# A graph layer's one-hot matrices: a third of the weight products on GpSimd, compare numbers in PSUM, three buffers

## The chip, the core and the metric

The kernel runs on one core of a Trainium2 chip. The metric is the device time of one execution in microseconds. The kernel before takes 516.95 us, the median of three runs (513.53 to 521.79).

## The reference, cut to what matters

There are 2048 nodes with 256 features and 67584 edges sorted by `dst`. The first layer sums weighted, normalised node rows over the edges; the second is a mixture of eight experts with two experts a token. The change touches only the first.

```python
edge_index = jnp.stack([src, dst])
# first layer: row = src, col = dst
gathered = edge_weight[:, None] * layernorm(x)[dst]
x = x + segment_sum(gathered, src, 2048) + node_vec1
# second layer: x + sum over the 2 best of 8 experts of weight * (gelu(LN(xt) @ W1) @ W2)
x = x + ffn(layernorm(x))
```

## The kernel before, in words

The kernel turns the edge sum into matrix products. It builds the weighted adjacency matrix, 2048 by 2048 in fp32, in slices of 64 `dst` nodes, and multiplies it with the normalised rows.

**Finding the edges.** The nodes are taken in 1024 pairs, 128 pairs to a round `q`, eight rounds. For each pair a GpSimd gather (L219, three of them: `win_s`, `win_d`, `win_w`) fetches the window of 128 edges that starts at the first edge of the pair; another gather (L200, `run`) and a ScalarE count (L209) find that start. VectorE makes two keys out of an edge (L252 to L255): its `src` modulo 128, and a number from 0 to 31 out of the `src` block and which of the two nodes it points at. TensorE transposes keys and weights (L263, L264), so that an edge of the window lies on each partition; ScalarE writes them out twice side by side as bf16 (`k2`, `w2`, L266 and L269). The fp32 weight is split into three bf16 parts, by subtractions on VectorE (L280) and casts on ScalarE (L281); `w2` holds the three parts.

**One-hots and the product.** A step `n`, of 32, takes 32 pairs, four steps to a round. `make_hots(n)` works on VectorE: L290 compares the first key with 0 to 127 and gives `hl` (128 partitions by 32 pairs by 128), L293 compares the second key with 0 to 31 and gives `eq` (32 by 32), and L297 multiplies `eq` with the three parts of the weight and gives `hr` (32 by 3 by 32). The numbers that are compared with are `iota_b`, bf16 in SBUF. `make_cols(n)` multiplies `hr` with `hl` on TensorE (L317, 96 products of 32 by 128, three adding up in PSUM), ScalarE copies the result out (L320), a DMA writes it to DRAM (L321), and every second step a DMA reads 128 `dst` nodes back as `ac` (L324). `dense` (L331) multiplies four such `ac` with the normalised rows, 16 fp32 matmuls for two blocks of output rows, and VectorE adds the result to `acc` (L336).

**Order.** All five engines run a list written out by hand (`manual_schedule`), each in its order. Step `n` of the loop issues `make_hots(n + 1)` first, then work for later rounds (L280 where `n % 4` is 0 or 1, L214 and L215 and the gathers where it is 1, L252 to L255 where it is 3), then the additions (L336) of the `dense` of the step before, then `make_cols(n)` and from `n = 9` on one `dense`, two at the end of a group of eight. `hl`, `eq` and `hr` have two buffers each, the product `pa` has three PSUM banks. GpSimd's queue holds only gathers in this stage. After the loop follow the last `dense` products, the routing of the tokens and the experts (L886 to L956), which the change leaves alone.

Of the kernel before, what the change touches and what calls it, by code (L numbers as in the profile page):

```python
# [9 lines left out]
F32 = mybir.dt.float32  # L10
BF16 = mybir.dt.bfloat16
# [3 lines left out]
OP = mybir.AluOpType  # L15
AX = mybir.AxisListType
PSUM = bass.MemoryType.PSUM
DRAM = bass.MemoryType.DRAM

P = 128  # L20
# [4 lines left out]
def kernel(  # L25
# [30 lines left out]
    nc = tc.nc  # L56
# [10 lines left out]
    RK = NB * GC  # L67
    GB = P // GC
    GH = GB // 2
# [19 lines left out]
    gnn = ctx.enter_context(ExitStack())  # L89
# [63 lines left out]
    iota_b = consts.tile([P, P], BF16, name="iota_b")  # L153
# [16 lines left out]

    cols_1 = gnn.enter_context(tc.tile_pool(name="cols_1", bufs=CB))
    ps_s = gnn.enter_context(tc.tile_pool(name="ps_s", bufs=2, space=PSUM))
    edges = gnn.enter_context(ExitStack())
    cols_0 = edges.enter_context(tc.tile_pool(name="cols_0", bufs=CB))
    pool = lambda name, bufs, **k: edges.enter_context(tc.tile_pool(name=name, bufs=bufs, **k))
# [51 lines left out]
    def block_stats(bn, mv, t, blocks):  # L227
        for b in blocks:
# [3 lines left out]

    prep = pool("prep", 2)
    keys = pool("keys", 3)
    hotl = pool("hotl", 2)
    hotr = pool("hotr", 2)
    rowsp = pool("rowsp", 3)
    ps_k = pool("ps_k", 1, space=PSUM)
    ps_a = pool("ps_a", 3, space=PSUM)
    two = lambda t, g, n: t[:, g * GH:(g + 1) * GH, None, :].to_broadcast([P, GH, n // 2, 2])  # L240
    pair = lambda n: iota_b[:, None, :n].rearrange("p o (n t) -> p o n t", t=2) \
                                        .to_broadcast([P, GH, n // 2, 2])
    parts = {}

# [39 lines left out]
    def make_hots(n):  # L284


        k2, w2, _ = parts[n // 4]
        g = n % 4
        hl = hotl.tile([P, GH, P], BF16, name="hl")
        nc.vector.tensor_tensor(hl.rearrange("p g (n t) -> p g n t", t=2),  # L290
                                two(k2[:, 0], g, P), pair(P), OP.is_equal)
        eq = hotr.tile([P, GH, RK], BF16, name="eq")
        nc.vector.tensor_tensor(eq.rearrange("p g (n t) -> p g n t", t=2),  # L293
                                two(k2[:, 1], g, RK), pair(RK), OP.is_equal)
        hr = hotr.tile([P, GH, 3, RK], BF16, name="hr")
        w = w2[:, g * GH:(g + 1) * GH].rearrange("p g i t -> p (g i) t")
        nc.vector.tensor_tensor(  # L297
            hr.rearrange("p g i (n t) -> p (g i) n t", t=2),
            eq[:, :, None, :].to_broadcast([P, GH, 3, RK]),
            w[:, :, None, :].to_broadcast([P, GH * 3, RK // 2, 2]), OP.mult)  # L300
        return hl, hr

    def make_cols(n, hl, hr):
# [37 lines left out]
    with tc.manual_schedule(engines=ALL):  # L341
# [24 lines left out]
        next_part(0, 2)  # L366
        turn_keys(1, f1)
        hots = {0: make_hots(0)}
        late = []
        NH = 2 * NB  # L370
        for n in range(NH):
            q = n // 4
            if n + 1 < NH:
                hots[n + 1] = make_hots(n + 1)
# [17 lines left out]
            g, k = divmod(n - 2 * CB - 1, 2 * CB)  # L392
# [14 lines left out]
            if n == 1:  # L407
# [4 lines left out]
                o = 0  # L412
# [10 lines left out]
                o = 0  # L423
# [68 lines left out]
    with tc.If(n_used < E):  # L492
# [11 lines left out]
        with tc.tile_pool(name="any", bufs=2) as anyp, tc.tile_pool(  # L504
            name="ps_any", bufs=2, space=PSUM
# [4 lines left out]
            with tc.For_i(0, E // P, 1) as t:  # L510
# [7 lines left out]
                g = anyp.tile([P, DX], F32, name="g")  # L518
# [593 lines left out]
```

## Time and profile before

| What | before |
|---|---|
| median of three runs | 516.95 us |
| span of the profiled execution | 517.6 us |
| busy TensorE, VectorE, ScalarE, GpSimd | 454.6, 282.2, 191.3, 149.9 us |
| first one-hot begins | 22.96 us |
| last product of one-hots begins | 209.15 us |
| last `dense` ends, experts begin | about 250 us |

In the profile PE is TensorE's matmul, PEld its weight load, DVE VectorE, ACT ScalarE, POOL GpSimd. A row of the groups gives the source line, the engine, the operation, out<-in with shapes and count, then the busy time in us and the mean duration of one in ns, then the idle time just ahead of these instructions and what ended it. A row of the timeline begins with the start and the duration in us. Rows of neighbours on one engine overlap by some 0.08 us, so what an instruction costs its engine is read from start to next start.

### The profile page before, as it was taken

What the parts mean: (1) busy time and instruction counts of PE and PEld (TensorE: products, weight loads), DVE (VectorE), ACT (ScalarE), POOL (GpSimd) and SP (SyncE); (2) the same over time, 40 slices, a digit from 0 to 9 for tenths busy, and PEclk for the clock granted to TensorE, in tenths of its full rate; (3) what the DMA queues carried; (4) which work ended last, traced back from release to release, by engine and by line L of the source; (5) the groups of instructions that cost most, each with busy time, mean ns of one, the idle gap of its engine ahead of it and who ended that gap; (6) DMA issues with size and microseconds to landing.
All of it is one profiled execution on the core that took longest, in us unless ns stands there. A gap on an engine that the chain in (4) does not pass through costs nothing.

```text
span 517.6 us, 12052 instructions
## 1 busy us (share of the span) xinstructions
PE 454.6 (88%) x4996; PEld 391.2 (76%) x4996; DVE 282.2 (55%) x591; ACT 191.3 (37%) x438; POOL 149.9 (29%) x126
## 2 busy tenths in 40 slices
PE   0154787999989999899999999999999999998993
PEld 0043675888768878778888888888888888887882
DVE  5698979998999899324857333322242312212111
ACT  1524777242343222025665323232334333233320
POOL 3505032341504000000042543443553444422231
PEclk9995698999989999999999999999999999999898
DMA  6214866766575657798421898998999677226510
GB/s 209 72 42 134 235 191 229 227 186 217 157 247 178 194 164 207 220 349 296 165 63 22 258 334 264 324 357 249 298 361 316 179 212 206 40 33 202 171 65 20
DMA packets 84356, 102.15 MB, mean 197 GB/s; under 512 B 8240, under 2 KB 74656, under 8 KB 82176
## 3 DMA queue, kind: packets, MB, share of 16 engines
q1 hardware_dynamic: 74832, 86.26, 51.5%
q0 software_dynamic: 7984, 13.91, 11.6%
q10 hardware_dynamic: 1472, 1.06, 0.7%
q8 instruction: 44, 0.72, 0.5%
q14 instruction: 24, 0.20, 0.1%
HBM read 75.18 MB, written 28.14 MB: 200 GB/s over the span
## 4 chain that ended last, share of the span: by engine, by line
PE 62%; DMA 19%; DVE 9%; issue 4%; ACT 4%; POOL 1%; SPq 0%; POOLq 0%; DVEq 0%; ACTq 0%
PE py L331 19%; PE py L935 16%; PE ph L921 15%; DMA xs<-xr_d,to_i 8%; PE pa L317 6%; DVE hl L290 3%; DMA ac<-ad 2%; DMA ad<-ar 2%; DVE hr L297 2%; PE px L742 2%; DMA y_d<-ys,to_i 2%; DMA out<-y_d 2%; DMA win_w<-in_edge_weight,at_i 1%; PE py L443 1%; PE px L886 1%
## 5 line engine op out<-in xcount | busy, mean ns | idle before, releaser
L331 PE MATMUL py<-xn_sb,ac 128*128 128x264 f32 x512 | 122.9, 396 | 4.4 <-DMA ac<-ad 3.0
L921 PE MATMUL ph<-xeT,w 128*128 128x256 f32 (+1 forms) x576 | 122.7, 372 | 2.5 <-PEq L1066 1.9
L935 PE MATMUL py<-w,hT 128*128 128x256 f32 x544 | 121.0, 379 | 0.0
L921 PEld LDWEIGHTS ph<-xeT,w 128*128 128x128 f32 x576 | 105.6, 192 | 16.9 <-issue 3.3
L331 PEld LDWEIGHTS py<-xn_sb,ac 128*128 128x128 f32 x512 | 96.9, 193 | 23.8 <-DMA ac<-ad 2.8
L923 ACT ACTIVATE hT<-ph,ec 128x256 f32<-128x256 f32 (+1 forms) x144 | 66.5, 462 | 125.3 <-PE ph L921 72.9
L935 PEld LDWEIGHTS py<-w,hT 128*128 128x128 f32 x544 | 101.8, 190 | 13.0
L943 POOL DMA_INDIRECT y_d<-ys,to_i x30 | 48.6, 1620 | 118.3 <-DVE ys L938 75.5
L290 DVE TENSOR_TENSOR hl<-k,iota_b 128x4096 bf16<-128x4096 bf16 x32 | 73.1, 2285 | 3.7 <-PE pa L317 3.7
L317 PE MATMUL pa<-hl,hr 128*32 128x128 bf16 x3072 | 56.9, 236 | 19.2 <-DVE hr L297 16.8
L317 PEld LDWEIGHTS <-hr 128*32 128x32 bf16 x3072 | 50.0, 106 | 28.3 <-DVE hr L297 18.4
L895 DVE TENSOR_SCALAR xeT<-px,ec 128x256 f32<-128x256 f32 (+1 forms) x38 | 18.4, 525 | 81.6 <-PE px L886 79.7
L297 DVE TENSOR_TENSOR hr<-eq,w 128x3072 bf16<-128x3072 bf16 x32 | 56.3, 1758 | 2.0 <-DVE eq L293 0.5
L938 DVE SCALAR_TENSOR_TENSOR ys<-py,wt,b2w 128x256 f32<-128x256 f32 x34 | 16.4, 484 | 74.5 <-PE py L935 59.4
L847 POOL DMA_INDIRECT xs<-xr_d,to_i x39 | 40.4, 1037 | 55.8 <-DVE r L613 43.5
L320 ACT COPY ar<-pa 128x512 f32<-128x512 f32 x64 | 35.4, 584 | 37.6 <-PE pa L317 36.4
L219 POOL DMA_INDIRECT win_s<-in_src,at_i x8 | 11.6, 1455 | 99.0 <-DVE r L280 94.8
L336 DVE TENSOR_TENSOR acc<-acc,py 128x528 f32<-128x528 f32 x32 | 22.2, 699 | 22.6 <-PE py L331 22.4
L910 ACT ACTIVATE b2w<-b,wt 128x256 f32<-128x256 f32 x36 | 16.3, 499 | 34.4 <-DVE wt L908 28.7
L263 PE MATMUL pk<-ident,f 128*128 128x128 f32 x16 | 4.7, 348 | 20.6 <-DVE f L254 16.3
L293 DVE TENSOR_TENSOR eq<-k,iota_b 128x1024 bf16<-128x1024 bf16 x32 | 21.9, 684 | 0.0
L263 PEld LDWEIGHTS pk<-ident,f 128*128 128x128 f32 x16 | 2.4, 158 | 22.8 <-issue 13.0
(193 smaller groups left out, 308.6 us busy)
## 6 DMA issues: line engine op xcount, KB each, us to landing
w<-in_L_ffn_W SPq DMA_DIRECT2D x40, 1024.0 KB, 9.3
ad<-ar SPq DMA_DIRECT2D x32, 512.0 KB, 4.5
ac<-ad SPq DMA_DIRECT2D x16, 1024.0 KB, 5.9
b<-in_L_ffn_b SPq DMA_DIRECT2D x20, 128.0 KB, 9.9
out<-y_d SPq DMA_DIRECT2D x4, 512.0 KB, 6.4
xr_d<-rec SPq DMA_DIRECT2D x1, 1300.0 KB, 6.2
y_d<-acc SPq DMA_DIRECT2D x1, 1280.0 KB, 5.9
acc<-in_x ACTq DMA_DIRECT2D x2, 512.0 KB, 5.9
```

Source lines behind the costliest of these rows:

```text
L290: nc.vector.tensor_tensor(hl.rearrange("p g (n t) -> p g n t", t=2), two(k2[:, 0], g, P), pair(P), OP.is_equal)
L293: nc.vector.tensor_tensor(eq.rearrange("p g (n t) -> p g n t", t=2), two(k2[:, 1], g, RK), pair(RK), OP.is_equal)
L297: nc.vector.tensor_tensor(hr.rearrange("p g i (n t) -> p (g i) n t", t=2), eq[:, :, None, :].to_broadcast([P, GH, 3, RK]), w[:, :, None, : ...
L317: nc.tensor.matmul(pa[j * RK:(j + 1) * RK, m, :], hr[:, g, i, :], hl[:, g, :], start=(i == 0), stop=(i == 2), tile_position=(0, j * RK))
L320: nc.scalar.copy(ar[:, m0:m0 + 4, :], pa)
L331: nc.tensor.matmul(pa[:, i, :DX], acs[g * CB + c][:, b + i, :], xn_sb[:, g * CB + c, :], start=(c == 0), stop=(c == CB - 1))
L336: nc.vector.tensor_add(acc[:, b:b + 2, :], acc[:, b:b + 2, :], pa[:, :, :DX])
L847: nc.gpsimd.indirect_dma_start(out=(sets[s.set][0] if into is None else into)[:, t, :], out_offset=None, in_=(xr_d if rows is None else ro ...
L921: nc.tensor.matmul(ph, w1[:, k, c * P:(c + 1) * P], xeT[:, k, :], start=(k == 0), stop=(k == KD - 1))
L923: nc.scalar.activation(hT[:, c, :s.n * P], ph, AF.Gelu, bias=ec[:, c:c + 1], scale=1.0)
L935: nc.tensor.matmul(py, hT[:, c, t * P:(t + 1) * P], w2[:, c, :], start=(c == 0), stop=(c == KH - 1))
L943: st = nc.gpsimd.indirect_dma_start(out=y_d[:, :], out_offset=bass.IndirectOffsetOnAxis(ap=tos[s.to][:, t:t + 1], axis=0), in_=ys, in_offs ...
```

## The change

GpSimd takes over the product of the one-hots with the third part of the weight; VectorE multiplies the first and second part in two instructions in place of one for all three. The numbers to compare with are copied once to a PSUM bank, as bf16 pairs moved as fp32, and both compares read them from there, so that of their two inputs one lies in SBUF. `hl`, `eq` and `hr` get three buffers; the PSUM bank is taken from `pa`, which keeps two. The aim is to take work off VectorE, to leave GpSimd room beside the compares, and to let the products on GpSimd end later without holding TensorE up. Nothing else in the order of TensorE, ScalarE and the DMA queues changes; in GpSimd's queue a product stands ahead of the gathers of its step.

```diff
+    ps_i = gnn.enter_context(tc.tile_pool(name="ps_i", bufs=1, space=PSUM))
+
+    iota_w = ps_i.tile([P, 512], F32, name="iota_t")[:, :P // 2]
+    nc.vector.tensor_copy(iota_w, iota_b.bitcast(F32))
+    iota_t = iota_w.bitcast(BF16)
...
-    hotl = pool("hotl", 2)
-    hotr = pool("hotr", 2)
+    hotl = pool("hotl", 3)
+    hotr = pool("hotr", 3)
...
-    ps_a = pool("ps_a", 3, space=PSUM)
+    ps_a = pool("ps_a", 2, space=PSUM)
...
-    pair = lambda n: iota_b[:, None, :n].rearrange("p o (n t) -> p o n t", t=2) \
+    pair = lambda n: iota_t[:, None, :n].rearrange("p o (n t) -> p o n t", t=2) \
...
-        w = w2[:, g * GH:(g + 1) * GH].rearrange("p g i t -> p (g i) t")
-        nc.vector.tensor_tensor(
-            hr.rearrange("p g i (n t) -> p (g i) n t", t=2),
-            eq[:, :, None, :].to_broadcast([P, GH, 3, RK]),
-            w[:, :, None, :].to_broadcast([P, GH * 3, RK // 2, 2]), OP.mult)
+        w = w2[:, g * GH:(g + 1) * GH]
+        for engine, i in ((nc.vector, 0), (nc.vector, 1), (nc.gpsimd, 2)):
+            engine.tensor_tensor(
+                hr[:, :, i, :].rearrange("p g (n t) -> p g n t", t=2),
+                eq.rearrange("p g (n t) -> p g n t", t=2),
+                w[:, :, i, None, :].to_broadcast([P, GH, RK // 2, 2]), OP.mult)
```

## Prediction

> **What bounds the kernel now.** I read the span in stages first, because the change touches only the steps between 23 and 211 us. The columns of the windows are the stretch, its length, then each engine's busy time.
>
> ```profile
> 28.00:54.00 26.00, 12.68 (x393) 11.29 (x394) 23.58 (x39) 9.02 (x18) 6.50 (x4) 0.73 0.41 107
> 54.00:88.00 34.00, 27.36 (x685) 24.55 (x684) 30.30 (x32) 26.69 (x64) 5.57 (x5) 0.85 0.67 208
> 88.00:140.00 52.00, 50.80 (x1023) 42.32 (x1024) 48.73 (x50) 18.96 (x46) 20.23 (x10) 0.97 0.66 207
> 140.00:177.00 37.00, 35.03 (x729) 28.90 (x728) 33.93 (x37) 11.50 (x30) 8.31 (x5) 0.95 0.68 209
> 177.00:211.00 34.00, 33.25 (x724) 27.42 (x724) 31.94 (x28) 8.80 (x17) 0.00 (x0) 1.00 0.63 184
> ```
>
> From 28 to 54 us VectorE is busy 23.6 of 26 us and TensorE half of it: VectorE bounds. From 88 us on TensorE is busy 119 of 123 us and bounds, but VectorE with 114.6 of 123 is only 7% behind. Whatever lengthens VectorE's step by more than some 0.4 us makes it the bound of all 32 steps; whatever shortens it pays in the first eight or nine only. The groups give the pieces of a step.
>
> ```profile
> L290 DVE TENSOR_TENSOR hl<-k,iota_b 128x4096 bf16<-128x4096 bf16 x32 | 73.1, 2285 | 3.7 <-PE pa L317 3.7
> L293 DVE TENSOR_TENSOR eq<-k,iota_b 128x1024 bf16<-128x1024 bf16 x32 | 21.9, 684 | 0.0
> L297 DVE TENSOR_TENSOR hr<-eq,w 128x3072 bf16<-128x3072 bf16 x32 | 56.3, 1758 | 2.0 <-DVE eq L293 0.5
> L331 PE MATMUL py<-xn_sb,ac 128*128 128x264 f32 x512 | 122.9, 396 | 4.4 <-DMA ac<-ad 3.0
> ```
>
> The first three lines hold 151 of VectorE's 168.5 busy us in the stage. 2285 against 684 ns for four times the elements: 0.52 ns an element and about 0.15 us fixed. VectorE waits for TensorE to give `hl` back 3.7 us in all. The next view, the timeline, shows what matters most here: how GpSimd and VectorE get on.
>
> ```profile
> 65.14 0.94 POOL L219 DMA_INDIRECT win_d<-in_dst,at_i  x1 [0.30 <-ACT ar L456]
> ...
> 87.43 2.28 DVE L290 TENSOR_TENSOR hl<-k,iota_b 128x4096 bf16<-128x4096 bf16 x1
> 87.54 2.99 POOL L219 DMA_INDIRECT win_s<-in_src,at_i  x1 [17.62 <-DVE r L280]
> ...
> 89.63 0.68 DVE L293 TENSOR_TENSOR eq<-k,iota_b 128x1024 bf16<-128x1024 bf16 x1
> ...
> 90.34 1.76 DVE L297 TENSOR_TENSOR hr<-eq,w 128x3072 bf16<-128x3072 bf16 x1
> ...
> 90.83 2.09 POOL L219 DMA_INDIRECT win_d<-in_dst,at_i  x1 [0.30 <-issue]
> ```
>
> With VectorE idle at 65 us a gather takes 0.94 us. The one at 87.54 us begins inside a compare and takes 2.99 us: it ends at 90.53, 0.90 us after the compare gave way to `eq` at 89.63. The one at 90.83 begins inside the product and ends at 92.92, 0.90 us after the next VectorE instruction starts at 92.02. So a VectorE instruction with two inputs in SBUF keeps GpSimd from its first read until that instruction ends, and GpSimd gets in at the very boundary, even where (`hl` to `eq`) VectorE follows on without a wait.
>
> **What the Trainium skill says.** "SBUF — State Buffer", section Who interferes with whom: a VectorE instruction with two SBUF inputs contends with a GpSimd instruction that reads SBUF, and whoever comes first holds the shared pair for its whole instruction while the other blocks. The rows above agree for GpSimd as the loser; no row of before shows VectorE as the loser, since a gather reads little. "VectorE: DVE Perf Modes", section The perf-mode tier table, puts `tensor_tensor` with any PSUM operand at one element a cycle, but its section Why PSUM operands drop a tier allows the packed two for 16-bit data. "Vector Engine (DVE) Microarchitecture Reference", section Performance modes, names for the packed mode only steps of one and 2-byte types, not the memory. The trace settles it only for fp32, where L280 takes 0.31 us from PSUM and 0.33 us from SBUF.
>
> **The change part by part.** From start to next start, VectorE's step is now 2.20 (`hl`, 104.85 to 107.05 us in the timeline) + 0.72 (`eq`, which the product waits for) + 1.67 (`hr`) = 4.59 us.
>
> *Two products in place of one.* A product of 1024 elements has the size of L293, 0.684 us by its row, about 0.60 from start to start where nothing is waited for (rows overlap by 0.08). Two are 1.20 against 1.67: 0.47 us saved in a step, 15 us in 32.
>
> *Compares from PSUM.* If the packed mode holds, they stay at 2.20 and 0.72. If not, 4096 elements at 1.04 ns (the 1x rate that L336 has: 699 ns for 528 elements is 0.15 fixed and 1.04 an element) are 2.14 us more and the 1024 of `eq` 0.53 more. I take the packed mode, and keep +2.67 us a step as the other end.
>
> *GpSimd's product.* The trace has none. "GPSIMD Engine Reference", section Performance versus the Vector engine, gives 4497 ns for a two-input operation of 2048 fp32 elements; in proportion 1024 take about 2.25 us, an estimate. Low end: its best loop at 1.8 cycles of 1.2 GHz an element, 1.54 us. High end: half as much again for an awkward access, 3.4 us. I take 2.25.
>
> *The wait it brings.* By the order of both engines, GpSimd's product waits for the same `eq` as VectorE's first product. A signal from VectorE to GpSimd takes 0.27 us (`at_i` ends at 87.27, its gather begins at 87.54), to VectorE itself 0.04, so VectorE's first product is under way when GpSimd asks. By the boundary seen above GpSimd gets in when it ends, 0.60 us later, while the second product stands next. Both read two SBUF inputs, so the second product waits out GpSimd's 2.25 us. Queued behind it on VectorE are the keys, the additions L336 and the next compare; TensorE's L317 waits for it too. A step becomes 4.59 - 0.47 + 2.25 = 6.37 us, +1.78. The compares of PSUM leave GpSimd free, but it asks at the wrong moment to use that.
>
> *Sum.* VectorE was busy 168.5 us between 28 and 211 us. With 30 steps there at +1.78 it is 222. Idle time of 14.5 us shrinks to about 7, since the waits for TensorE (3.7) and for L269 behind it (3.6) go. 229 against 183 is +46, and the two steps before 28 us add 3.5: +49.5. The work after 211 us is the same. 517 + 49 = 566 us.
>
> *At nothing.* The copy to PSUM at the start (64 elements, like L156 at 0.22 us) lies in VectorE's wait of 3.85 us for the first run. The third buffer and the two banks for `pa` move only waits of TensorE, which has 1 us to spare in a step of 6.4. Gathers beside the compares fall from 2 to 3 us to 0.95, on a queue with time left: four products and four gathers are 13 of 25 us.
>
> **The rivals.**
> *Free overlap (ends not slower).* GpSimd reads in the gaps and VectorE loses nothing. For it: only GpSimd is seen to lose. Against: the skill's whole-instruction rule. Then VectorE saves 0.47 in the eight steps that it bounds, 3.8 us, and the third buffer takes the one wait of 2.9 us at 64 us; with two `pa` banks TensorE pays perhaps 0.7 us more at each of four places where ScalarE's copies come late (as at 130 us). -6.7 to -3.9: about 511 us.
> *A milder clash.* GpSimd gets in only after the second product, and the 16 steps with keys or indices next wait 2.25 us: 36 - 15 = +21 of VectorE; or both share at half rate, +1.2 - 0.47 in each step, +23. 168.5 + 22 + 7 is 197.5 against 183: about 532 us. Against it: the entry at the boundary.
> *Compares at one element a cycle.* +2.67 - 0.47 = 2.20 in 32 steps is 70, less 7 of idle time: 580 us, and with the block on top above 640. For it the tier table, against it the two sections beside it.
>
> **How the numbers follow.** Block between the products 0.46, free overlap 0.30, milder clash 0.12, slow compares 0.12. Free overlap is within 2% but for a small part with more gain than I can find: faster 0.05, same 0.26, slower 0.69. The range starts at 507, below the free overlap. A GpSimd product of 3.4 us would give 602 and one of 1.54 us 544; I end at 595, which leaves out most of the slow compares and the last of the long products.
>
> **What would show it.** Right: in the profile after, L303 (the products) on VectorE has rows of about 0.68 us and rows of near 3 us, or gaps of above 2 us ahead of the second one, while GpSimd's L303 runs; `hl` stays at 2.28 us; TensorE waits for VectorE from 88 us on, with a step above 6 us. Wrong: VectorE's products all at 0.68 us beside GpSimd's and a step of 5.3 us as before (free overlap), delays on L280 or L252 in place of the second product (milder clash), or `hl` above 4 us. A GpSimd product far from 2.25 us moves the time by 32 us for each us.

## The result, and the profile after

The changed kernel takes 544.11 us (median of four runs, 542.83 to 545.88) against 517.24 us before (four runs, 513.53 to 521.79): a ratio of 1.052, 95% interval 1.048 to 1.056. (Every ratio here leaves out runs more than 1.5% above the fastest of the same kernel; on the first and the third chip of the experiments that takes 32 of 47 and 27 of 71 runs from the kernel before and at most 3 from a variant, so a ratio there can be up to 1.4 points above that of the medians.) It is slower by 27 us. All of that lies in the stage with the one-hots: the very last matmul of their products starts at 237.6 us in place of 210.4, and what follows takes as long as before (306.5 and 307.2 us).

The windows of the changed kernel, at the stretches shown of before and one more. Columns: stretch, length, busy time of TensorE's matmuls, its weight loads, VectorE, ScalarE and GpSimd, then the granted clock, the DMA share and GB/s.

```profile
28.00:54.00 26.00, 9.98 (x316) 9.07 (x320) 23.65 (x36) 7.93 (x16) 11.63 (x8) 0.85 0.26 74
54.00:88.00 34.00, 26.44 (x666) 24.21 (x655) 33.57 (x34) 24.36 (x57) 17.15 (x10) 0.82 0.66 192
88.00:140.00 52.00, 44.73 (x902) 36.90 (x902) 51.59 (x57) 18.56 (x47) 26.83 (x17) 0.97 0.67 197
140.00:177.00 37.00, 30.34 (x661) 25.07 (x661) 36.72 (x38) 11.61 (x29) 16.49 (x11) 0.95 0.52 162
177.00:211.00 34.00, 28.39 (x564) 23.22 (x563) 32.72 (x31) 8.35 (x20) 12.59 (x6) 0.95 0.51 146
211.00:238.00 27.00, 23.41 (x451) 18.88 (x451) 25.29 (x23) 4.65 (x9) 9.51 (x4) 0.94 0.68 210
```

From 54 us on VectorE is busy nearly without a break (33.6 of 34 us, 51.6 of 52, 36.7 of 37), and TensorE, which had 119 busy us of the 123 from 88 to 211 us, now has 103.5. The bound has passed to VectorE, although a part of its work was taken away. The groups of the same kernel say which work grew.

```profile
L295 DVE TENSOR_TENSOR hl<-k,iota_t 128x4096 bf16<-128x4096 bf16 x32 | 72.9, 2278 | 0.0
L298 DVE TENSOR_TENSOR eq<-k,iota_t 128x1024 bf16<-128x1024 bf16 x32 | 21.7, 679 | 0.0
L303 DVE TENSOR_TENSOR hr<-eq,w 128x1024 bf16<-128x1024 bf16 x64 | 92.3, 1483 | 1.1
L303 POOL TENSOR_TENSOR hr<-eq,w 128x1024 bf16<-128x1024 bf16 x32 | 74.5, 2328 | 104.0 <-DVE eq L298 101.4
L323 PE MATMUL pa<-hl,hr 128*32 128x128 bf16 x3072 | 59.3, 240 | 38.0 <-ACT ar L326 25.6
```

The compares, now with one input in PSUM, cost what they did (2278 and 679 ns; 2285 and 684 before). VectorE's two products take 92.3 us together, where the one product of all three parts took 56.3: a third less work, and 36 us more time. VectorE's busy time over the whole run rose by 35.5 us, from 282.2 to 317.7, so nothing else grew. GpSimd's 74.5 us of products are new; its gathers got shorter.

The timeline of the changed kernel, first a step as most are, then one that escapes. An x2 joins VectorE's two products, with nothing but their overlap between them.

```profile
110.85 3.04 DVE L303 TENSOR_TENSOR hr<-eq,w 128x1024 bf16<-128x1024 bf16 x2
110.96 2.38 POOL L303 TENSOR_TENSOR hr<-eq,w 128x1024 bf16<-128x1024 bf16 x1 [4.77 <-DVE eq L298]
...
113.81 0.31 DVE L285 TENSOR_TENSOR r<-pk,w 128x128 f32<-128x128 f32 x1
...
114.16 0.41 ACT L286 CAST w<-r 128x256 bf16<-128x256 f32 x1 [3.01 <-DVE r L285]
114.47 1.06 ACT L326 COPY ar<-pa 128x512 f32<-128x512 f32 x2
...
115.09 1.52 PE L323 MATMUL pa<-hl,hr 128*32 128x128 bf16 x96 [0.92 <-ACT ar L326]
...
123.68 0.94 POOL L224 DMA_INDIRECT win_w<-in_edge_weight,at_i  x1 [0.31 <-issue]
...
124.55 1.29 DVE L303 TENSOR_TENSOR hr<-eq,w 128x1024 bf16<-128x1024 bf16 x2
...
125.76 0.70 DVE L342 TENSOR_TENSOR acc<-acc,py 128x528 f32<-128x528 f32 x1
126.07 1.95 POOL L303 TENSOR_TENSOR hr<-eq,w 128x1024 bf16<-128x1024 bf16 x1
```

At 110.85 us the pair takes 3.04 us. Taken singly, its first product lasts 0.69 us and its second 2.43. GpSimd's product begins at 110.96, while the first is under way, and ends at 113.34, 1.80 us after that first one ended. So it got in between the two. At 124.55 the same pair takes 1.29 us: GpSimd's product stands behind four gathers in its queue (the third is shown) and comes at 126.07, beside L342 and the next `hl`, which read PSUM. Of the 32 pairs in the timeline 29 take about 3.04 us and three 1.29. A clash so costs 3.04 - 1.29 = 1.75 us, and 29 of them 50.8 us. The pair at 124.55 us also shows that VectorE does not wait for GpSimd's result by the program: it is over before GpSimd's product begins.

The rows between show how it spreads. The fp32 remainder L285 stands behind the pair on VectorE; ScalarE's cast L286 waits for it (3.01 us idle), ScalarE's copies L326 stand behind the cast, and TensorE waits for them because both `pa` banks are full. Hence TensorE's idle time of 38.0 us ahead of L323 is put down to ScalarE for 25.6 us, with VectorE at its root here. The line of the kernel before:

```profile
L317 PE MATMUL pa<-hl,hr 128*32 128x128 bf16 x3072 | 56.9, 236 | 19.2 <-DVE hr L297 16.8 <-ACT ar L320 2.3
```

### The profile page after: what moved, and what is told of

Same layout as the page of the kernel before. It is cut to its first block, busy times and chain, and to the rows that moved or that the text cites. A ratio compares the mean times of both kernels' runs of the same rounds, so it can differ in the third digit from the quotient of the medians.

```text
span 544.1 us, 12131 instructions
## 1 busy us (share of the span) xinstructions
PE 459.0 (84%) x4996; PEld 394.2 (72%) x4996; DVE 317.7 (58%) x624; ACT 191.7 (35%) x438; POOL 205.2 (38%) x158
## 4 chain that ended last, share of the span: by engine, by line
PE 35%; DMA 12%; issue 4%; DVE 1%; ACT 1%; SPq 0%; POOL 0%; POOLq 0%; DVEq 0%; ACTq 0%
PE py L941 15%; PE ph L927 14%; DMA xs<-xr_d,to_i 8%; PE py L337 4%; DMA y_d<-ys,to_i 2%; DMA out<-y_d 2%; PE px L892 1%; DMA so_far<-out,to_i 1%; PE px L748 1%; DMA out<-ys,to_i 0%; SPq L1085 0%; POOL out L962 0%; DVE acc L342 0%; ACT L929 0%; POOLq L1114 0%
## 5 line engine op out<-in xcount | busy, mean ns | idle before, releaser
L337 PE MATMUL py<-xn_sb,ac 128*128 128x264 f32 x512 | 124.6, 400 | 4.4 <-DVE acc L342 3.0
L337 PEld LDWEIGHTS py<-xn_sb,ac 128*128 128x128 f32 x512 | 98.1, 196 | 24.5 <-DVE acc L342 3.8
L303 POOL TENSOR_TENSOR hr<-eq,w 128x1024 bf16<-128x1024 bf16 x32 | 74.5, 2328 | 104.0 <-DVE eq L298 101.4
L303 DVE TENSOR_TENSOR hr<-eq,w 128x1024 bf16<-128x1024 bf16 x64 | 92.3, 1483 | 1.1
L323 PE MATMUL pa<-hl,hr 128*32 128x128 bf16 x3072 | 59.3, 240 | 38.0 <-ACT ar L326 25.6
L323 PEld LDWEIGHTS <-hr 128*32 128x32 bf16 x3072 | 52.4, 108 | 47.3 <-issue 27.8
L295 DVE TENSOR_TENSOR hl<-k,iota_t 128x4096 bf16<-128x4096 bf16 x32 | 72.9, 2278 | 0.0
L326 ACT COPY ar<-pa 128x512 f32<-128x512 f32 x64 | 35.7, 583 | 38.3 <-PE pa L323 34.7
L342 DVE TENSOR_TENSOR acc<-acc,py 128x528 f32<-128x528 f32 x32 | 22.2, 698 | 21.8 <-PE py L337 21.8
L286 ACT CAST w<-r 128x256 bf16<-128x256 f32 x16 | 6.6, 410 | 53.0 <-DVE r L285 53.0
L268 PE MATMUL pk<-ident,f 128*128 128x128 f32 x16 | 4.6, 352 | 23.1 <-DVE f L259 19.5
L298 DVE TENSOR_TENSOR eq<-k,iota_t 128x1024 bf16<-128x1024 bf16 x32 | 21.7, 679 | 0.0
```

Source lines behind the costliest of these rows:

```text
L303: engine.tensor_tensor(hr[:, :, i, :].rearrange("p g (n t) -> p g n t", t=2), eq.rearrange("p g (n t) -> p g n t", t=2), w[:, :, i, None, ...
L323: nc.tensor.matmul(pa[j * RK:(j + 1) * RK, m, :], hr[:, g, i, :], hl[:, g, :], start=(i == 0), stop=(i == 2), tile_position=(0, j * RK))
L326: nc.scalar.copy(ar[:, m0:m0 + 4, :], pa)
L337: nc.tensor.matmul(pa[:, i, :DX], acs[g * CB + c][:, b + i, :], xn_sb[:, g * CB + c, :], start=(c == 0), stop=(c == CB - 1))
L342: nc.vector.tensor_add(acc[:, b:b + 2, :], acc[:, b:b + 2, :], pa[:, :, :DX])
```

## The experiments

The experiments ran on three chips, and each ratio is to the kernel before on the same one. On the first (`eq` first, VectorE alone, zeros, numbers in SBUF) the kernel before took 526.0 us in the median, on the second (`eq` first with SBUF, two banks, `eq` first with two buffers, half the product) 517.22, on the third (the last four) 526.07. By the medians of all runs the ratios on the first are, in this order, 0.995, 0.999, 0.993 and 1.046, and on the third, in the order below, 0.995, 0.998, 0.985 and 0.998. Differences of 1% and less on these two chips are therefore not safe; the loss of 5 to 6% is.

### GpSimd asks one instruction earlier

```diff
+        eq = hotr.tile([P, GH, RK], BF16, name="eq")
+        nc.vector.tensor_tensor(eq ..., OP.is_equal)
         hl = hotl.tile([P, GH, P], BF16, name="hl")
         nc.vector.tensor_tensor(hl ..., OP.is_equal)
-        eq = hotr.tile([P, GH, RK], BF16, name="eq")
-        nc.vector.tensor_tensor(eq ..., OP.is_equal)
```

> The changed kernel with one move: eq is compared ahead of hl, so that GpSimd's product is released beside the 2.2 us compare from PSUM and not beside VectorE's two products. Theory (GpSimd takes the shared read port at the boundary between VectorE's two products and the second one waits out its hold): all 64 products on VectorE at 0.69 us, hl stays at 2.28 us, a step of VectorE 4.1 us without keys and additions, time 508 to 516 us, no slower than before. Rival (the late result of GpSimd, or the PSUM banks taken from pa, hold TensorE up): 535 us or more with short products. Rival (a compare with one SBUF input is blocked as well): hl near 4 us, 540 us.

Measured: 523.43 us, ratio 1.006 (1.003 to 1.009). The timeline of this kernel:

```profile
109.51 2.27 DVE L298 TENSOR_TENSOR hl<-k,iota_t 128x4096 bf16<-128x4096 bf16 x1
109.73 1.94 POOL L303 TENSOR_TENSOR hr<-eq,w 128x1024 bf16<-128x1024 bf16 x1 [4.80 <-DVE eq L295]
...
111.71 1.27 DVE L303 TENSOR_TENSOR hr<-eq,w 128x1024 bf16<-128x1024 bf16 x2
```

The long compare, with one input in PSUM, and GpSimd's product run side by side, and neither is longer for it. VectorE's pair then takes 1.27 us. Nothing was changed but the moment at which GpSimd asks, and nearly all of the 5.2% is gone. The clash is left in four steps, where GpSimd's product comes late, behind gathers. One of them, and the group (688 ns would be no clash at all, as a later run shows):

```profile
44.57 3.15 DVE L303 TENSOR_TENSOR hr<-eq,w 128x1024 bf16<-128x1024 bf16 x2
44.61 1.95 POOL L303 TENSOR_TENSOR hr<-eq,w 128x1024 bf16<-128x1024 bf16 x1
```

```profile
L303 DVE TENSOR_TENSOR hr<-eq,w 128x1024 bf16<-128x1024 bf16 x64 | 48.2, 792 | 0.0
```

In this step it is VectorE's first product that is held: it lasts 2.55 us, although it had begun 0.04 us before GpSimd's. In two other steps GpSimd's product begins some 0.2 us after one of VectorE's (at 143.85 and 165.13 us), isn't delayed (1.95 us each), and the pair takes 3.33 and 3.32 us. All three follow directly on a gather, and went first from behind; in the changed kernel the product that had waited for `eq` began 0.11 us after VectorE's (110.96 and 110.85 us) and was locked out. So the earlier start in the trace doesn't tell who goes first, and the boundary is not the only way in. Why is not shown. The hold is longer here, 1.87 to 2.05 us in place of 1.75.

### No product on GpSimd

All three parts in one VectorE instruction, with PSUM compares, three buffers and two banks as in the changed kernel:

```diff
-        for engine, i in ((nc.vector, 0), (nc.vector, 1), (nc.gpsimd, 2)):
-            engine.tensor_tensor(hr[:, :, i, :] ..., OP.mult)
+        nc.vector.tensor_tensor(hr ..., w of all three parts, OP.mult)
```

> The changed kernel with all three parts multiplied on VectorE in one instruction as before; compares from PSUM, three buffers and two banks for pa stay. Theory: 512 to 520 us, since nothing but GpSimd's product costs; hr at 1.76 us, hl at 2.28 us; gathers all near 0.95 us unless they meet a product. Rival (the two banks for pa cost): 525 us or more, TensorE waiting for ScalarE's copies.

Measured: 525.37 us, ratio 1.008 (1.003 to 1.013). The rest of the change therefore makes about 0.8 of the 5.2 points, at most 1.3 by the interval, and the product on GpSimd, once it doesn't clash, is some 0.3% better than this (1.006 against 1.008), which can't be told from nothing: the intervals overlap. In microseconds this run and the first lie above what was expected of them (512 to 520 and 508 to 516), and so does the next, on a chip where the kernel before lies at 526. TensorE waits 13.3 us for ScalarE's copies here, so the rival of the two banks needed the run of its own that stands below.

GpSimd fills the third part with zeros in place of multiplying it:

```diff
-        for engine, i in ((nc.vector, 0), (nc.vector, 1), (nc.gpsimd, 2)):
+        for engine, i in ((nc.vector, 0), (nc.vector, 1)):
...
+        nc.gpsimd.memset(hr[:, :, 2, :], 0.0)
```

> The changed kernel with GpSimd writing zeros over the third part in place of multiplying, at the end of the same step, so the third part of the weight is left out of the result; GpSimd still writes as many elements and TensorE still waits for it, but it reads nothing from SBUF and has no compare to wait for. Theory (the reads clash): VectorE's products 0.69 us, 508 to 516 us. Rival (any GpSimd work beside VectorE's products, or TensorE's wait for GpSimd, costs): products of 1.5 us and more or time above 530 us.

Measured: 522.25 us, ratio 1.003 (1.000 to 1.006). Its groups:

```profile
L303 DVE TENSOR_TENSOR hr<-eq,w 128x1024 bf16<-128x1024 bf16 x64 | 41.4, 688 | 3.1
L307 POOL MEMSET hr<- 128x1024 bf16 x32 | 30.0, 961 | 54.8 <-PE pa L324 46.3 <-issue 8.3
```

VectorE's products are at 688 ns, all of them. In part that is because the fill need not wait for `eq` and comes at other times; but where they meet, they don't clash either: a fill from 189.25 to 190.20 us lies beside a pair from 189.53 to 190.82 us, and both keep their length (0.95 and 1.29 us). This agrees with what the Trainium skill, "SBUF — State Buffer", section Who interferes with whom, says: a VectorE instruction with two SBUF inputs contends with a GpSimd instruction that reads SBUF, not with one that only writes.

### What the numbers in PSUM are worth

The changed kernel with both compares reading `iota_b` in SBUF again, and then the same with `eq` first:

```diff
-    pair = lambda n: iota_t[:, None, :n] ...
+    pair = lambda n: iota_b[:, None, :n] ...
```

> The changed kernel with the compares reading SBUF again (the copy in PSUM is made but not read). Theory: GpSimd asks after eq and is done before the next hl in nearly every step, so PSUM gains little in this order: 544 to 552 us, with longer gathers as the one difference. Rival (PSUM compares carry the change): 560 us or more, with GpSimd's products at 4 us and more.

Measured: 550.42 us, ratio 1.061 (1.054 to 1.068). The gathers of the windows are back at 1.3 to 1.7 us in the mean (0.94 to 0.97 in the changed kernel). The compares are held at times too: `hl` has a mean of 2399 ns in place of 2278, `eq` of 789 in place of 679.

> The kernel with eq first, and the compares reading SBUF again (the copy in PSUM is made but not read). GpSimd's product is now released just as the 2.2 us compare begins. Theory (a VectorE instruction with two SBUF inputs locks GpSimd out whole, then the product takes the boundary): the product waits out hl and enters ahead of VectorE's first product, so one product a step waits 1.75 us as in the changed kernel; ratio to before 1.045 to 1.065. Rival (the order alone is the cure, PSUM is not needed): as with PSUM, 1.00 to 1.01.

Measured: 550.43 us, ratio 1.064 (1.059 to 1.070). Its timeline:

```profile
111.43 2.29 DVE L298 TENSOR_TENSOR hl<-k,iota_b 128x4096 bf16<-128x4096 bf16 x1
111.66 3.86 POOL L303 TENSOR_TENSOR hr<-eq,w 128x1024 bf16<-128x1024 bf16 x1 [2.59 <-DVE eq L295]
113.64 3.04 DVE L303 TENSOR_TENSOR hr<-eq,w 128x1024 bf16<-128x1024 bf16 x2
```

The compare begins first and reads SBUF twice, so GpSimd stands still until it ends at 113.72. Then it gets in ahead of VectorE's pair, and the pair takes 3.04 us again. The two edits need each other: `eq` first without PSUM gains nothing (1.064), and PSUM without `eq` first is the changed kernel (1.052). Whether PSUM is worth anything in that order isn't settled: 1.052 and 1.061 come from two chips, their intervals meet, and by the medians the second is 1.046.

### Half the product on GpSimd

```diff
+        for engine, i, a, b in ((nc.vector, 0, 0, GH), (nc.vector, 1, 0, GH),
+                                (nc.gpsimd, 2, 0, GH // 2), (nc.vector, 2, GH // 2, GH)):
+            engine.tensor_tensor(hr[:, a:b, i, :] ..., OP.mult)
```

> The changed kernel, its order kept, with GpSimd multiplying 16 of the 32 pairs and VectorE the other 16 in one more instruction of 512 elements (about 0.35 us). Theory (the second product waits as long as GpSimd reads): the hold falls from 1.75 us to about 0.9 us, so a step saves 0.85 - 0.35 = 0.5 us, and the ratio falls from 1.052 to about 1.02 to 1.04; GpSimd's product about 1.0 us after its entry. Rival (a fixed price for each meeting): hold still 1.75 us, ratio 1.06.

Measured: 528.46 us, ratio 1.021 (1.016 to 1.027). Its timeline, where VectorE's x3 is the two products of 1024 elements and one of 512:

```profile
111.47 2.50 DVE L304 TENSOR_TENSOR hr<-eq,w 128x1024 bf16<-128x1024 bf16 x3
111.58 1.50 POOL L304 TENSOR_TENSOR hr<-eq,w 128x512 bf16<-128x512 bf16 x1 [4.67 <-DVE eq L298]
```

Where GpSimd's product comes late, as at 70.90 us, the three take 1.63 us, so VectorE is held 2.50 - 1.63 = 0.87 us for half the product, against 1.75 for the whole. The hold goes with the length of GpSimd's instruction (two lengths were run); a fixed price for each meeting is ruled out. The loss follows: 0 to 0.8% with no clash or few, 2.1% with half, 5.2% with the whole.

### The buffers and the banks

Two banks for `pa` in the kernel before, nothing else:

```diff
-    ps_a = pool("ps_a", 3, space=PSUM)
+    ps_a = pool("ps_a", 2, space=PSUM)
```

> The kernel before with two PSUM banks for pa in place of three, nothing else. Theory (what is left over in the kernels without the clash, +0.3 to +0.8%, comes of the bank given away): ratio 1.003 to 1.01, with TensorE waiting for ScalarE's copies some 10 us in place of 2.3. Rival (the bank is free): 0.997 to 1.002.

Measured: 517.77 us, ratio 0.999 (0.997 to 1.002). Its line:

```profile
L317 PE MATMUL pa<-hl,hr 128*32 128x128 bf16 x3072 | 56.7, 238 | 21.9 <-ACT ar L320 12.5 <-DVE hr L297 7.9 <-issue 1.5
```

Against the line of the kernel before above, TensorE's waits for ScalarE's copies rise from 2.3 to 12.5 us and those for VectorE's `hr` fall from 16.8 to 7.9; the sum hardly moves (19.2 and 21.9), and the time doesn't.

`eq` first, with two buffers of one-hots in place of three:

```diff
-    hotl = pool("hotl", 3)
-    hotr = pool("hotr", 3)
+    hotl = pool("hotl", 2)
+    hotr = pool("hotr", 2)
```

> The kernel with eq first, with two buffers each for hl, eq and hr as before the change. Theory (TensorE bounds, a third buffer only lets VectorE run ahead): within 0.5% of the kernel with three buffers, ratio to before 1.00 to 1.012. Rival (GpSimd's late product needs the third buffer): above 1.015, with VectorE waiting for TensorE or GpSimd ahead of its compares.

Measured: 512.28 us, ratio 0.988 (0.983 to 0.994), below the expected 1.00 to 1.012: apparently a gain, and apparently the third buffer's fault that the first experiment had none. Since the two had run on different chips, the last four went to one chip together: `eq` first with three buffers and with two, the kernel before with three, and VectorE alone with two.

> The changed kernel with eq compared ahead of hl, as before, with three buffers of one-hots; run again beside its two-buffer form, so that the two share one chip. If the third buffer costs: 1.003 to 1.008 of the time before, and over 1.2% above the two-buffer form, with some 8 us of TensorE's waits in its matmuls put down to issue. If the difference so far was one of chips: 0.988 to 0.995 here, level with the two-buffer form.

Measured: 523.36 us, ratio 1.000 (0.997 to 1.003), between the two expectations. Its line:

```profile
L323 PE MATMUL pa<-hl,hr 128*32 128x128 bf16 x3072 | 61.3, 236 | 23.1 <-ACT ar L326 11.7 <-issue 6.9 <-DVE hr L303 4.3
```

> The same order with two buffers of one-hots. Third buffer costs: 0.983 to 0.994 of the time before and over 1.2% below the three-buffer form in this call. Chips: level with the three-buffer form within 0.5%.

Measured: 524.95 us, ratio 1.002 (0.999 to 1.005). So the two are level, and by these ratios neither beats the kernel before here. The suspicion of the third buffer falls, and with it the gain: the same code is 0.988 on one chip and 1.002 on another, with intervals that don't meet. What differs can be seen but not explained. In this run TensorE has gaps within its one-hot products for which the trace shows no cause ("issue"), 9.3 us of them; on the other chip there were 2.1. The chip alone doesn't decide that: the kernel before with three buffers, on this same chip, has 2.8. The granted clock differs as well: 0.72 from 54 to 70 us and 0.69 from 70 to 88 us, on the other chip 0.79 and 0.81, and from 28 to 88 us this run gets through 862 of the one-hot matmuls, the other through 935. Neither is shown to be the cause. The line of this kernel:

```profile
L323 PE MATMUL pa<-hl,hr 128*32 128x128 bf16 x3072 | 61.1, 236 | 26.2 <-ACT ar L326 13.0 <-issue 9.3 <-DVE hr L303 3.9
```

The kernel before with three buffers:

```diff
-    hotl = pool("hotl", 2)
-    hotr = pool("hotr", 2)
+    hotl = pool("hotl", 3)
+    hotr = pool("hotr", 3)
```

> The kernel before with hotl and hotr at three buffers and nothing else changed. If a third buffer costs by itself, whatever VectorE does: 1.01 to 1.02, and TensorE's idle in its matmuls moves from VectorE hr to issue and to ScalarE's copies. If it costs only along with the compares from PSUM, the two banks or the freed GpSimd: 0.997 to 1.003.

Measured: 517.92 us, ratio 0.992 (0.989 to 0.996). Neither expectation holds: the third buffer doesn't cost, it helps a little. Its line:

```profile
L317 PE MATMUL pa<-hl,hr 128*32 128x128 bf16 x3072 | 60.6, 240 | 18.6 <-DVE hr L297 13.3 <-issue 2.8 <-ACT ar L320 2.0
```

VectorE's wait for TensorE ahead of `hl`, 3.7 us before, is gone (0.0). At 0.8%, some 4 us, the gain is about as large; that the one makes the other is argued from the size and wasn't tested. A rival stands: 517.92 us is what the kernel before takes on the other chip (517.22), so the third buffer may only have spared this chip whatever makes the kernel before take 526 us there. It ran on no second chip.

> The changed kernel with all three products on VectorE in one instruction, compares from PSUM, two buffers of one-hots. With three buffers it took 1.008. If the third buffer costs some 1.5%: 0.99 to 0.997, and what is left of e10's gain over it is what GpSimd's product is worth. If buffers don't matter here: 1.005 to 1.012 again.

Measured: 525.27 us, ratio 1.004 (1.001 to 1.007). Against `eq` first with two buffers on the same chip (1.002) GpSimd's product is again worth 0.2%, with intervals that overlap. It lies between the two expectations, and settles neither.

The best version against the kernel before is thus the kernel before with three buffers of one-hots and nothing else, by 0.8% on the one chip where it ran. `eq` first with two buffers was 1.2% better on another.

## Why the prediction was right or wrong

**The direction and its mechanism: right, and shown.** The step that decided was that GpSimd enters at the boundary between VectorE's two products and that the second waits out GpSimd's whole instruction. The rows at 110.85 us show it, and the order experiment shows the moment to be the cause: the same product on the same engine, asked for one instruction earlier, costs 0.6% on one chip and nothing on another. The half product shows that the hold goes with the length. Two of the prediction's readings were off without consequence: the signal from VectorE to GpSimd takes 0.15 us here and not 0.27, still more than VectorE's own 0.04, and the 151 us of its three lines are those of all 32 steps, one of which lies before 28 us. The likeliest time was 566 us and the time is 544, within the range. The rule from the Trainium skill's "SBUF — State Buffer", section Who interferes with whom, that whoever is first holds the shared pair for a whole instruction holds here with VectorE as the loser, which no row of before could show; but "first" isn't the earlier start in the trace, as the rows at 44.57 us of the order experiment show.

**GpSimd's product: mis-sized.** The prediction took 2.25 us, in proportion to an fp32 figure. Where nothing disturbs it, the bf16 product takes 1.94 to 1.95 us, and it holds VectorE for 1.75. The 2.33 us of its group's mean contain some 0.4 us in which GpSimd itself waits for the boundary, and would have seemed to confirm the wrong figure.

**"+1.78 in each step": mis-sized in the count too.** Three steps escape, because the product stands behind four gathers there and comes too late to clash. The prediction named the gathers in the queue, but only to show that there was time left. With the measured terms its sum reads: 29 clashes x 1.75 = 50.8 us, less 32 x 0.47 = 15 us saved, is +35.8 of VectorE's time, where 35.5 was measured and 53.5 + 3.5 predicted. The term for VectorE's idle time was right: 14.5 us idle of the 183 from 28 to 211 us become 6.5 of the 210 from 28 to 238 us, where "about 7" was written. 35.8 - 8 is +28; the span grew by 26.5. Nearly the whole miss of 22 us is the hold (0.5 us x 29 = 14.5) and the three steps (3 x 2.25 = 6.8).

**The compares from PSUM: right.** They take 2278 and 679 ns with one operand in PSUM, 2285 and 684 with both in SBUF, so these bf16 compares keep the packed mode. Slow compares as a rival falls.

**"At nothing": right for what was listed.** The copy to PSUM takes 0.22 us ahead of the first one-hot, which begins at 23.12 us (22.96 before). The gathers of the windows fell to 0.94 to 0.97 us. The bank given away costs nothing by itself (0.999). TensorE's 1 us to spare in a step was used up where L285 is queued behind the blocked pair, but with VectorE busy 203.6 of the 210 us from 28 to 238 this delays nothing of VectorE's.

**The rival of free overlap: its mechanism false, its price open.** VectorE does lose. Where the order experiment brings about what that rival described, the time with three buffers isn't 511 us but level with before to 0.6% above it, on two chips that have the kernel before at 526. With two buffers, on the one chip that has it at 517, the time was 512.28 us, near the rival's figure. The 6 us were to come from the steps that VectorE bounds and from the third buffer. VectorE is indeed relieved, by 11 us of busy time from 28 to 238 us (161.7 in the repeated order run, 172.7 with VectorE alone, on one chip), but TensorE's idle time ahead of its one-hot products is no smaller than with the old order: 23.1 us there, 18.6 in the kernel before with three buffers, on the same chip. With two banks it waits for ScalarE's copies (11.7 us in place of 2.0) and for the gaps without a cause (6.9). That these keep the relief from paying is argued from the waits and wasn't tested. The prediction had put 0.7 us at four places, 2.8 us, on the banks. Three banks with the clash away weren't tried, since the copied numbers hold the third bank.

**The milder clash: false.** L285 and L257 behind the pair start late, but the pair itself carries the block. That its 532 us lay nearer to 544 than the 566 of the true mechanism is luck and says nothing for it.

## What to carry to other kernels

Before work goes from VectorE to GpSimd, look at which VectorE instruction is running when GpSimd becomes ready, and what stands next: in these traces, where both read two inputs in SBUF, GpSimd entered at their boundary and the next one was held for 1.75 of the 1.94 us of GpSimd's instruction. Moving the producer one place earlier, so that GpSimd's share runs beside an instruction with an operand in PSUM, removed nearly all of a 5% loss here, and neither the PSUM operand nor the order did so alone. And ask first what the relief can bring: TensorE was busy for 119 of 123 us in most of this stage, and the work that moved without a clash brought nothing that these runs can tell.

## What the hardware showed that was not expected

- GpSimd multiplies 1024 bf16 elements per partition in 1.94 us, 14% below the estimate from fp32, and 512 in 1.07; it fills 1024 in 0.96 us. VectorE's product of 1024 takes 0.69.
- A block at the boundary costs VectorE 1.75 us although the blocking instruction takes 1.94 alone; for half the size it is 0.87 against 1.07. About 0.2 us of GpSimd's instruction lie outside the hold. Where GpSimd's product followed a gather and began up to 0.2 us after VectorE's, it still went first, and the cost was 1.87 to 2.05 us.
- VectorE's compares with bf16 numbers in PSUM take what they take from SBUF (2278 and 2285 ns for 4096 elements), and run beside a GpSimd product with neither held.
- One and the same kernel stood at 0.988 of the kernel before on one chip and at 1.002 on another, and the kernel before itself at 517 and 526 us. A gain of 1% measured on one chip is not yet one.
